# Second rows of the last sums: from VectorE to ScalarE and GpSimd in the closing blocks of an expert layer

## The chip, the cores and the metric

One core of one Trainium2 chip runs the whole program. The metric is the device time of one execution in microseconds; the time before is the median of three runs. A profile is one further execution, recorded by the hardware profiler; its times in this document are microseconds from the start of its span.

## The reference

Four layers follow each other on x of 8 sequences x 512 tokens x 256 features, all in float32:

```python
x = x + attn_a(layernorm(x))      # 16 heads of 64, slopes on the distance, causal
x = x + ffn(layernorm(x))
x = x + attn_b(layernorm(x))      # 8 heads of 128, rotary, causal
x = x + ffn(layernorm(x))

# ffn(x): 8 experts, each token goes to 2 of them
h   = rmsnorm(x) * norm_w
vals, idx = top_k(h @ gate_w.T + gate_b, 2)
wts = softmax(vals)
y_e = mlp2_e(swiglu(mlp1_e(h)))   # for the two experts e of the token
ffn = x + sum(wts[k] * y[idx[k]] for k in (0, 1))
```

The last line of the last layer is what this document is about: to each token's row two expert rows are added, each multiplied by the token's own weight.

## The kernel before, in words

A layer's tokens lie as 8 sequences of 4 tiles, 128 tokens on the partitions and 256 features along them. In an expert layer the 4096 tokens, each with two experts, are sorted by expert into 71 blocks of 128 rows (`TOTAL`). For each block n the loop `Experts.run` issues, in steps:

- `gather` (L939): GpSimd fetches the block's 128 rows from DRAM by an indirect DMA, four blocks ahead (`LEAD`); after step 66 there is none left to fetch;
- `turn_rows` (L953, L961): TensorE transposes, ScalarE copies;
- `first` (L982 to L998), two steps later: TensorE multiplies with the expert's weights, VectorE adds the bias from PSUM (L993), ScalarE takes a sigmoid (L994), and VectorE does three more operations in SBUF (L996, L997, L998);
- `turn_act` (L1007, L1012), then `second` (L1021 to L1033), six steps later (`DEPTH`): TensorE's second product, VectorE's bias from PSUM (L1032, "y"), and GpSimd's indirect DMA that scatters the block's rows to DRAM, to the places of their tokens (L1033, "scatter").

The tokens are sorted in two groups, the first group being sequences 0 to 5. The first 55 blocks (`TOUCHED`) hold all rows of that group, so its results may be read back while the remaining blocks run. The program names blocks by group and number; the second group's numbers 0 to 29 are blocks 41 to 70. This document says y25 or scatter 25 for number 25 of the second group (block 66), and y29 or scatter 29 for the last block.

Reading back goes by halves: two tiles of one sequence, here named by sequence and first tile, 0_0, 0_2, 1_0 and so on to 5_2 for the first group. `collect` (L1078) reads both rows of every token of a half, 256 KB for the first rows and 256 KB for the second. `add` (L1118) makes the sums: for each tile VectorE adds weight times first row to x and then weight times second row to x, two operations of 128x256 that depend on each other. `store` (L1246) sends the half to the output. For half k the three are put at steps n, n + 4 and n + 6 of the loop, with n = 61 + 3k // 2; so the sums of 0_0 and 0_2 stand at 65 and 66, those of 1_0 at 68, and those of 5_2 at 81.

The results of sequences 6 and 7 (second group) can be read only when all scatters are in DRAM. These eight reads, 6_0 to 7_2, are issued last, half on SP's queue (first rows) and half on ScalarE's queue (second rows). In the program text they stand ahead of the sums of 4_0 to 5_2 (steps 77 to 81), and the sums and stores of sequences 6 and 7 close the program.

TensorE's order is written out by hand. On the other engines a scheduler orders the instructions by its own estimates; `keep_in_program_order` holds some of them in the order of the text. Each engine runs its queue in order, and so do SP's queue and ScalarE's queue of DMA issues: whatever waits at the head holds what is behind it. DMAs issued by SP and ScalarE share eight completion semaphores in turn, so that each waits for the one eight places before it. Read buffers are shared: 3_0 takes over the buffer of 1_0, 5_0 that of 3_0, and so on.

Of the kernel before, what the change touches and what calls it, by code (L numbers as in the profile page):

```python
# [41 lines left out]
ALU = mybir.AluOpType  # L42
# [35 lines left out]
TOTAL = (2 * NB * T + SPARE) // P  # L78
# [4 lines left out]
LEAD = 4  # L83
# [10 lines left out]
def layers(  # L94
# [24 lines left out]
    nc = tc.nc  # L119
# [70 lines left out]
    def iota(shape, pattern, name, multiplier=0, base=0, dtype=F32):  # L190
        t = const.tile(shape, dtype, tag=name, name=name)
        nc.gpsimd.iota(
            t,
            pattern=pattern,
            base=base,
            channel_multiplier=multiplier,
            allow_small_or_imprecise_dtypes=True,
        )
        return t
# [6 lines left out]
    tiles = iota([P, 2, NB * NT], [[32, 2], [1, NB * NT]], "tiles", 0, 64)  # L206
# [73 lines left out]
    class Attention:  # L280
# [75 lines left out]
        def scores(self, b, g, n):  # L356
# [4 lines left out]
            if n == 0:  # L361
                rows = []
                for i in range(nh):
                    rows.append(
                        (
                            work.tile([P, PACKED], F32, tag="S", bufs=4, name=f"S_{key}_{i}"),
                            small.tile([P, NT], F32, tag="nm", bufs=4, name=f"nm_{key}_{i}"),
                            small.tile([P, NT], F32, tag="sum", bufs=4, name=f"sum_{key}_{i}"),
                        )
                    )  # L370
                self.S[b, g] = rows
                if kind == "a":
                    add = []
                    for i in range(nh):
                        a = work.tile([P, T], F32, tag="tmp", bufs=3, name=f"ali_{key}_{i}")
                        nc.gpsimd.tensor_scalar(  # L376
                            a, alibi_sb, SLOPES[nh * g + i], 1.0, ALU.mult, ALU.mult
                        )
                        add.append(a)
                    self.add[b, g] = add, -1.0  # L380
                else:
                    self.add[b, g] = [mask_sb], -1.0 / DB
            add, scale = self.add[b, g]
            bank = S_BANKS[n]
            rows = P // nh
# [158 lines left out]
    class Experts:  # L544
# [191 lines left out]
        def blocks_up(self, i, out, counts, add):  # L736

            whole = self.rt(i, [P, NE], "whole", I32)
            nc.vector.tensor_scalar_add(whole, counts, float(add))
            nc.vector.tensor_scalar(  # L740
                whole, whole, 7, 7, ALU.logical_shift_right, ALU.logical_shift_left
            )
            nc.vector.tensor_copy(out, whole)
# [365 lines left out]
                self.read(engines[k], b, got[:, k], k * PLANE + m * P, len(tiles) * P)  # L1109
            self.got[b, tiles[0]] = got  # L1110

        def add(self, b, tiles):
            got = self.got[b, tiles[0]]
            for n, t in enumerate(tiles):
                m = b * NT + t
                xs = X[b][:, t, :]
                for k in range(2):
                    made = nc.vector.scalar_tensor_tensor(  # L1118
                        xs, got[:, k, n, :], self.R["w"][k][:, m : m + 1], xs, ALU.mult, ALU.add
                    )  # L1120
                    tc.keep_in_program_order(made)


# [71 lines left out]
    def flush(left, exp):  # L1195

        turns = (0, 2, 2, 2, 3, 5, 8, 10, 12, 14)
        aside = {}
        for n, piece in zip(turns, left, strict=True):
            aside.setdefault(n, []).append(piece)  # L1200
        for n, piece in zip((16, 18, 20, 22, 25, 28), exp.sorting(1), strict=True):
            aside[n] = [piece]
        return aside
# [7 lines left out]
    att_b, exp_b = Attention("b"), Experts("f2")  # L1211
# [9 lines left out]
    aside = flush(layer(att_a, exp_a, more), exp_a)  # L1221
    aside.setdefault(6, []).append(weights_b)
    aside[done] = [lambda: exp_a.fetch(0)]
    for k, tag in enumerate(("xT", "PT")):
        tt = (2 * k, 2 * k + 1)
# [17 lines left out]
    aside = flush(layer(att_b, exp_b, more), exp_b)  # L1243

    def store(b, tiles, engine):
        engine.dma_start(  # L1246
            out=by_tokens(out[b])[:, tiles[0] : tiles[-1] + 1, :],
            in_=X[b][:, tiles[0] : tiles[-1] + 1, :],
        )
# [7 lines left out]
    for k, (b, tt) in enumerate(halves):  # L1257
        n = done + 3 * k // 2
        tag = ("xT", "PT")[k % 2] if k not in (8, 9) else "qk"
        aside.setdefault(n, []).append(  # L1260
            lambda b=b, tt=tt, tag=tag: exp_b.collect(b, tt, tag, both_queues)
        )
        aside.setdefault(n + 4, []).append(lambda b=b, tt=tt: exp_b.add(b, tt))
        aside.setdefault(n + 6, []).append(lambda b=b, tt=tt: store(b, tt, nc.sync))
    end = TOTAL + DEPTH
    exp_b.run(aside)
# [75 lines left out]
```

## Time and profile before

| | us |
|---|---|
| median of three runs (2226.54 to 2229.31) | 2227.3 |
| the profiled execution, whole | 2239.6 |
| its span, first to last instruction | 2237.8 |
| VectorE's sums in this layer (L1118), 64 operations | 0.480 each (median) |
| the last scatter (L1033), start | 2219.56 |
| the reads of sequences 6 and 7, first issue | 2222.59 |
| the last sum, end | 2234.34 |

How to read the profile: PE is TensorE, PEld its weight loads, DVE VectorE, ACT ScalarE, POOL GpSimd, SP the queue that issues DMAs; ACTq and SPq mark DMA issues on the queue of ScalarE and of SP. A row in order of time has the start, the duration, the engine, the line, the operation and the names of what it writes and reads, the count of merged instructions, and in brackets the idle time of the engine before it and what ended that. Over its span the granted clock of TensorE was 0.993.

### The profile page before, as it was taken

To read this page: it belongs to the slowest core of one execution; us is meant where nothing else is said; L and a number is where in the kernel's file an instruction comes from. 1 tells how busy PE (TensorE), PEld (TensorE's weight loads), DVE (VectorE), ACT (ScalarE), POOL (GpSimd) and SP (SyncE) were. 2 spreads that over 40 slices of the span, in tenths; PEclk is the share of its full clock that TensorE was granted. 3 is DMA by queue.
4 is the path that set the end of the run, shared out by engine and by line. 5 is a ranking of instruction groups with operands and counts; after the bars stand their busy time and mean duration, and the time that the engine had idled before them with its cause. 6 is when DMAs were issued, how large, how long until landed. Compare 5 with 4: busy or idle time off the path is not lost.

```text
span 2237.8 us, 33567 instructions
## 1 busy us (share of the span) xinstructions
PE 2190.3 (98%) x10513; PEld 1429.2 (64%) x10513; DVE 1586.9 (71%) x4817; ACT 961.6 (43%) x2784; POOL 967.1 (43%) x1337
## 2 busy tenths in 40 slices
PE   8999999999999999999999999999999999999995
PEld 5666666666666666656666666666666666665663
DVE  4566666666666687687787676777777678968768
ACT  4555555555555555323324334434444433333331
POOL 5443434243433333266654343333434343356662
PEclk9999999999999999999999999999999999999997
DMA  7100000000000000232220010100101010042237
GB/s 248 39 15 15 6 24 1 30 1 29 1 29 1 29 6 29 99 106 84 90 76 29 10 39 10 39 29 19 48 6 43 6 34 1 19 139 78 85 101 252
DMA packets 78382, 108.80 MB, mean 49 GB/s; under 512 B 9568, under 2 KB 64000, under 8 KB 78208
## 3 DMA queue, kind: packets, MB, share of 16 engines
q1 hardware_dynamic: 62656, 67.58, 9.4%
q0 software_dynamic: 13632, 37.24, 5.4%
q8 instruction: 87, 1.43, 0.3%
q10 hardware_dynamic: 1920, 1.84, 0.3%
q14 instruction: 87, 0.71, 0.1%
HBM read 67.02 MB, written 39.60 MB: 48 GB/s over the span
## 4 chain that ended last, share of the span: by engine, by line
PE 88%; DVE 7%; issue 2%; ACT 1%; POOL 1%; SPq 1%; DMA 1%; DVEq 0%; ACTq 0%; POOLq 0%
PE pp_b L337 10%; PE hp_f L982 9%; PE pp_a L337 9%; PE op_a L476 6%; PE sp_b L395 6%; PE sp_a L395 6%; PE tp_a L449 6%; PE op_b L476 6%; PE yp_a L494 5%; PE yp_b L494 5%; PE vp_a L318 4%; PE y_f L1021 4%; PE vp_b L318 4%; PE tp_b L449 3%; PE gtp_f L953 1%
## 5 line engine op out<-in xcount | busy, mean ns | idle before, releaser
L417 ACT ACTIVATE S_a<-S_a,nm_a 128x512 f32<-128x512 f32 (+3 forms) x512 | 280.1, 548 | 313.7 <-DVE nm_a L407 309.9
L350 POOL TENSOR_TENSOR qk_b<-qk_b,rot_b 128x512 f32<-128x512 f32 x128 | 163.0, 1274 | 453.1 <-DVE qk_b L349 427.7
L376 POOL TENSOR_SCALAR ali_a<-alibi 128x512 f32<-128x512 f32 x128 | 79.3, 620 | 454.9 <-DVE nm_a L407 443.1
L982 PE MATMUL hp_f<-we,hT_f 128*128 x544 | 257.8, 596 | 4.3 <-DVE u_f L993 2.9
L417 ACT ACTIVATE S_b<-S_b,nm_b 128x512 f32<-128x512 f32 (+3 forms) x256 | 142.9, 559 | 241.1 <-DVE nm_b L407 233.4
L407 DVE CUSTOM_DVE_ANT_0 S_a<-sp_a,ali_a 128x512 f32<-128x512 f32 (+3 forms) x512 | 215.9, 487 | 30.7 <-PE sp_a L395 30.7
L434 POOL TENSOR_SCALAR S_a<-S_a,sum_a 128x384 f32<-128x384 f32 x378 | 203.1, 554 | 34.6 <-DVE sum_a L428 25.0
L1033 POOL DMA_INDIRECT y_f<-y_f,row_f x142 | 143.4, 1010 | 114.1 <-DVE y_f L1032 59.2
L407 DVE CUSTOM_DVE_ANT_0 S_b<-sp_b,mask 128x512 f32<-128x512 f32 (+3 forms) x256 | 119.4, 485 | 77.1 <-PE sp_b L395 76.7
L395 PE MATMUL sp_b<-qk_b 128*128 128x512 f32 (+3 forms) x512 | 169.7, 434 | 2.6 <-POOL qk_b L350 2.5
L449 PE MATMUL tp_a<-ident,S_a 128*128 128x128 f32 x1280 | 166.2, 276 | 5.4 <-DVE O_a L484 3.3
L939 POOL DMA_INDIRECT g_f<-h_all_f,token_f x142 | 144.4, 1017 | 59.4 <-issue 39.6
L449 PEld LDWEIGHTS tp_a<-ident,S_a 128*128 128x128 f32 x1280 | 141.3, 142 | 36.8 <-issue 21.3
L994 ACT ACTIVATE u_f<-u_f 128x256 f32<-128x256 f32 x142 | 59.2, 417 | 238.0 <-DVE u_f L993 179.5
L476 PE MATMUL op_a<-PT_a,V_a 128*64 128x384 f32 (+3 forms) x1024 | 156.0, 442 | 3.3 <-ACT S_a L417 2.2
L1021 PEld LDWEIGHTS y_f<-we,aT_f 128*128 128x128 f32 x568 | 108.8, 193 | 77.1 <-issue 59.6
L395 PE MATMUL sp_a<-qk_a 64*128 64x512 f32 (+3 forms) x1024 | 155.5, 443 | 0.9 <-DVE qk_a L354 0.9
L1021 PE MATMUL y_f<-we,aT_f 128*128 x568 | 148.6, 385 | 3.8 <-ACT aT_f L1012 3.7
L459 ACT COPY PT_a<-tp_a 128x512 f32<-128x512 f32 (+1 forms) x320 | 139.1, 496 | 29.4 <-PE tp_a L449 27.6
L476 PE MATMUL op_b<-PT_b,V_b 128*128 128x512 f32 (+3 forms) x512 | 148.7, 433 | 0.0
L993 DVE TENSOR_TENSOR u_f<-hp_f,be 128x512 f32<-128x512 f32 x142 | 98.2, 691 | 59.5 <-PE hp_f L982 20.5
L982 PEld LDWEIGHTS hp_f<-we,hT_f 128*128 128x128 f32 x544 | 92.7, 190 | 73.1 <-issue 66.3
(205 smaller groups left out, 4454.8 us busy)
## 6 DMA issues: line engine op xcount, KB each, us to landing
h_all_f<-hn_f SPq DMA_DIRECT2D x64, 128.0 KB
xm_f<-x_mid_f SPq DMA_DIRECT2D x16, 512.0 KB
yg_f<-y_f SPq DMA_DIRECT2D x32, 256.0 KB
yg_f<-y_f SPq DMA_DIRECT2D x56, 128.0 KB
we<-w_dram SPq DMA_DIRECT2D x8, 512.0 KB
x_mid_f<-x SPq DMA_DIRECT2D x8, 512.0 KB
x_mid_f<-xm_f SPq DMA_DIRECT2D x8, 512.0 KB
x<-x_in_dram SPq DMA_DIRECT2D x7, 512.0 KB
```

The lines of the kernel that those rows point to most:

```text
L318: nc.tensor.matmul(vp[:, k, :], lhsT=self.xT[b][:, c, t * P : (t + 1) * P], rhs=wv[:, c, q * 2 * P : (q + 1) * 2 * P], start=(c == 0), sto ...
L337: nc.tensor.matmul(pp, lhsT=w[:, c, g * P : (g + 1) * P], rhs=self.xT[b][:, c, :], start=(c == 0), stop=(c == NC - 1),)
L350: nc.gpsimd.tensor_tensor(qk[:, j, :], qk[:, j, :], rot, ALU.add)
L395: nc.tensor.matmul(sp[i][:, at[it] : at[it] + w], lhsT=qk[r, 0, it * P : (it + 1) * P], rhs=qk[r, 1, 0:w], start=True, stop=True,)
L407: nc.vector.tensor_tensor_reduce(out=s, in0=sp[i][:, at[it] : at[it] + w], in1=add[i][:, T - w : T], scale=scale, scalar=float(np.finfo(np ...
L417: nc.scalar.activation(s, s, AF.Exp, bias=nm[:, it : it + 1], scale=-1.0, accum_out=sums[:, it : it + 1],)
L434: eng.tensor_scalar(s, s, sums[:, it : it + 1], 1.0, ALU.mult, ALU.mult)
L449: nc.tensor.transpose(tp[:, o : o + P], S[:, S_OFF[it] + jt * P : S_OFF[it] + (jt + 1) * P], ident,)
L476: nc.tensor.matmul(op[i * cols : (i + 1) * cols, jt * P : T], lhsT=v[:, jt, c0 : c0 + cols], rhs=PT[i][:, P_OFF[jt] : P_OFF[jt] + T - jt * P],
L494: nc.tensor.matmul(yp[:, 0:D], lhsT=o[:, c, t * P : (t + 1) * P], rhs=wo[:, half * HALF + c, :], start=(c == 0), stop=(c == HALF - 1),)
L982: nc.tensor.matmul(hp, lhsT=h[:, c * P : (c + 1) * P], rhs=we_sb[:, bass.DynSlice(wat + c * 2 * FI, 2 * FI)], start=(c == 0), stop=(c == N ...
L1021: nc.tensor.matmul(yp, lhsT=aT[:, c * P : (c + 1) * P], rhs=we_sb[:, bass.DynSlice(wat + NC * 2 * FI + c * D, D)], start=(c == 0), stop=(c ...
```

## The change

`add` gets a flag. Where it is set, the second row of each tile is multiplied by its weight in place by ScalarE, and GpSimd adds the product to x. The first row stays with VectorE. The flag is set for halves whose sums stand at step 67 (`TOTAL - LEAD`) or later, from where on no more rows are gathered: 1_0 to 5_2, ten halves of two tiles. The sums of 0_0 and 0_2, those of sequences 6 and 7, and the other expert layer stay as they are.

```diff
-        def add(self, b, tiles):
+        def add(self, b, tiles, shared=False):
             got = self.got[b, tiles[0]]
             for n, t in enumerate(tiles):
                 m = b * NT + t
                 xs = X[b][:, t, :]
                 for k in range(2):
-                    made = nc.vector.scalar_tensor_tensor(
-                        xs, got[:, k, n, :], self.R["w"][k][:, m : m + 1], xs, ALU.mult, ALU.add
-                    )
+                    row, w = got[:, k, n, :], self.R["w"][k][:, m : m + 1]
+                    if k and shared:
+
+                        made = nc.scalar.mul(row, row, w)
+                        tc.keep_in_program_order(made)
+                        nc.gpsimd.tensor_tensor(xs, xs, row, ALU.add)
+                        continue
+                    made = nc.vector.scalar_tensor_tensor(xs, row, w, xs, ALU.mult, ALU.add)
                     tc.keep_in_program_order(made)
...
-        aside.setdefault(n + 4, []).append(lambda b=b, tt=tt: exp_b.add(b, tt))
+        aside.setdefault(n + 4, []).append(
+            lambda b=b, tt=tt, n=n: exp_b.add(b, tt, n + 4 >= TOTAL - LEAD)
+        )
```

## The prediction

> **What bounds the kernel now.** I read the page first, then the busy time by stretches of the end, then the order of time on each engine there. The edit acts only in the second expert layer, from block 67 of 71 on, so the first 2196 us stay as they are. The stretches of the end (PE, PEld, DVE, ACT, POOL busy with counts, then granted clock, DMA share, GB/s):
>
> ```profile
> 2170.00:2190.00 20.00, 20.00 (x82) 12.75 (x82) 15.14 (x37) 6.53 (x20) 12.51 (x13) 1.00 0.67 189
> 2190.00:2210.00 20.00, 18.25 (x71) 11.03 (x69) 18.83 (x47) 5.16 (x16) 5.83 (x6) 1.00 0.77 249
> 2220.00:2238.00 18.00, 0.00 (x0) 0.00 (x0) 13.78 (x32) 0.00 (x0) 0.54 (x1) 0.54 0.78 257
> ```
>
> Until 2190 TensorE is full. After it the sums (L1118) come in and VectorE is full: 18.83 of 20 us, then alone. ScalarE and GpSimd are nearly empty there, but the DMA engines are at 0.78. The order of time shows what ends it (POOL, then DVE, ACT's queue, SP's queue):
>
> ```profile
> 2211.69 1.16 POOL L1033 DMA_INDIRECT y_f<-y_f,row_f  x1 [2.45 <-DVE u_f L996]
> 2215.36 0.97 POOL L1033 DMA_INDIRECT y_f<-y_f,row_f  x1 [0.30 <-issue]
> 2219.56 0.97 POOL L1033 DMA_INDIRECT y_f<-y_f,row_f  x1 [1.74 <-DVE y_f L1032]
> ...
> 2218.87 0.42 DVE L1032 TENSOR_TENSOR y_f<-y_f,be 128x256 f32<-128x256 f32 x1
> 2219.20 15.14 DVE L1118 SCALAR_TENSOR_TENSOR xm_f<-yg_f,wt_f,xm_f 128x256 f32<-128x256 f32 x33
> ...
> 2222.59 2.11 ACTq L1078 DMA_DIRECT2D yg_f<-y_f  x4
> 2230.71 4.05 ACTq L1246 DMA_DIRECT2D out_dram<-xm_f  x2
> ...
> 2222.69 1.92 SPq L1078 DMA_DIRECT2D yg_f<-y_f  x4
> 2227.00 5.91 SPq L1246 DMA_DIRECT2D out_dram<-xm_f  x5
> ```
>
> Two chains meet. One is VectorE's row of sums without a gap. The other is: last y (2218.87), its scatter by GpSimd (2219.56 to 2220.53), landing, and the eight reads of sequences 6 and 7, which wait for every scatter (2222.59, 2.06 us after the scatter's end). Of the 33 sums the last 16 belong to these reads and start at about 2226.9. At 2227.00 SP issues a store that carries a wait for the first of the reads; SP had been free since 2224.61. So the first pair lands about 4.35 us after its issue, just when VectorE comes to it. VectorE and the reads are therefore near a tie: relief for VectorE alone does not move the end unless the last scatter moves as well. From the last sum's end (2234.34) to the end of the span are 3.46 us of store.
>
> **The change part by part.** Twelve halves (two tiles of a sequence) belong to the first stage; halves 1_0 to 5_2, ten of them, change. For each of their 20 tiles one VectorE sum goes, one ScalarE multiplication and one GpSimd addition come.
>
> *VectorE.* The two sums of one tile depend on each other. Start to start they take 0.40 and 0.52 us in turn (33 in 15.14 us is 0.46 on average); first rows alone do not depend on each other, 0.40. So 20 x 0.52 = 10.4 us leave VectorE, 12 of the 20 ahead of the last y, 8 behind it.
>
> *ScalarE.* 20 multiplications of 128x256. Nearest row: the sigmoid of that shape, 0.42 us, so 8.4 us, in two places. Twelve stand between sigmoids and copies, where ScalarE waits 2 to 3 us per block (below): hidden; the copies for the next block come 0.8 us later, and TensorE uses them about 2 us later.
>
> ```profile
> 2200.97 0.42 ACT L994 ACTIVATE u_f<-u_f 128x256 f32<-128x256 f32 x1 [2.79 <-DVE u_f L993]
> ```
>
> The other eight (halves 4_0 to 5_2) stand, in the changed program's order, behind ScalarE's four reads of sequences 6 and 7, and these wait for the last scatter. They cannot start before the reads are out, although their data are there long before. No table load is added.
>
> *GpSimd.* 20 additions. The same form stands in the first layer, undisturbed:
>
> ```profile
> L299 POOL TENSOR_TENSOR x<-x,bout x32: 717/722/732, 13.7 to 795.6; 128x256 f32<-128x256 f32 x32
> ```
>
> They are put between the scatters: after that of y25 come two additions (2_2), scatters 26 and 27, two additions (3_0), scatter 28, two additions (3_2), scatter 29, then eight more. So the last scatter, which gates the reads, now queues behind six additions, each of which waits for ScalarE and VectorE.
>
> *The shared port.* Does a GpSimd addition hold up VectorE? The trace has the case in the attention, a GpSimd operation with a sum beside it:
>
> ```profile
> 1199.53 0.83 POOL L434 TENSOR_SCALAR S_b<-S_b,sum_b 128x384 f32<-128x384 f32 x1
> 1199.83 0.81 DVE L1118 SCALAR_TENSOR_TENSOR xm_f<-yg_f,wt_f,xm_f 128x256 f32<-128x256 f32 x1
> ...
> L1118 DVE SCALAR_TENSOR_TENSOR xm_f<-yg_f,wt_f,xm_f x64: 468/580/809, 1139.8 to 1833.9; 128x256 f32<-128x256 f32 x64
> L1118 DVE SCALAR_TENSOR_TENSOR xm_f<-yg_f,wt_f,xm_f x64: 472/480/486, 2188.0 to 2233.9; 128x256 f32<-128x256 f32 x64
> ```
>
> The sum takes 0.81 instead of 0.48 and ends 0.28 after the GpSimd operation: +0.33 us. At the end of the kernel, with only scatters beside them, no sum is over 0.486. The Trainium skill (SBUF — State Buffer, section "SBUF: two separate sides") states the rule behind it, against this change: a VectorE operation with two SBUF inputs and a GpSimd operation that reads SBUF exclude each other, and the loser "fully blocks". By the rule taken whole, each meeting costs the loser 0.72 us; by the row 0.33, because the start of a sum still overlaps. I take the row and keep 0.72 as the upper end. L997 and L998 also have two SBUF inputs; L993 and L1032 read PSUM and can run beside an addition. The skill's GPSIMD Engine Reference (section "Engine selection") has GpSimd about twice as slow as VectorE with two inputs, that is 0.8 to 1.0 us by this trace's VectorE rows; the row of 0.722 is used.
>
> *Sum.* (a) Up to y25 three changed halves pass (1_0, 1_2, 2_0). A block with four sums takes 3.75 us on VectorE (L993 at 2196.44 to L993 at 2200.19); two second sums less is 1.04, three times 3.1. Two of the six additions meeting a VectorE operation give back 0.6. Scatter 25 starts at 2211.69 - 2.5 = 2209.2. (b) From there to scatter 29 GpSimd has four scatters at 1.27 (0.97 and 0.30 of issue) = 5.1 us and six additions at 0.72 = 4.3, plus 0.2 each for meetings = 1.2: start at 2219.8, against 2219.56. VectorE itself gets to y29 some 5 us earlier than before, for nothing: GpSimd has taken its place. Ends: undisturbed and the full 3.1 earlier, 2218.0; with additions of 1.1 us, 2220.9. Reads then go out at 2222.8, +0.2 us. (c) VectorE is done with the first stage and waits for the pair, 4.35 us, then runs 16 sums, 7.4 us. In this time the last eight additions come: they can start 2.5 us after the reads go out and need at least 5.8 us, so six of them run beside the sums: 6 x 0.33 = +2.0 us (ends: 0, and 6 x 0.72 = 4.3). (d) The stores: that of 6_0 stands on SP's queue ahead of those of 4_0 to 5_2 in the changed order, so eight stores of 256 KB follow the reads where seven did. 0.25 MB at the 257 GB/s above is 1.0 us; I take it as hidden under the longer row of sums, up to 1.0 otherwise.
>
> Sum: +0.2 + 2.0 = +2.2 us. The profiled execution took 2239.6 us (span 2237.8 and 1.8 around it), which becomes 2241.8. The median of the runs shown is 2227.3, 12.3 below the profiled one; the difference is carried over: 2229.5.
>
> **The rivals.** *Faster: VectorE's relief reaches the end.* For it: VectorE is the chain's end for 40 us and loses 10.4. If the additions fit between the scatters, the last scatter follows y29 at about 2214, 5.4 us earlier, and the eight late additions disturb nothing: 2227.3 - 5.4 = 2221.9. Against it: the six additions are ahead of the last scatter in one queue, and (b) leaves at most 1.5 us. It decides if scatter 29 starts before 2216.
>
> *Slower: GpSimd becomes the end.* Each addition waits for two engines and for the port. If one in this stretch takes 1.1 us instead of 0.72, scatter 29 starts at 2220.9 (+1.3); with the late six at the full 0.72 (+4.3) and the eighth store exposed (+1.0) it is +6.6: 2233.9. The point is about 0.9 us per addition together with a whole block per meeting. For it: the queue order and the 0.81 row. Against it: VectorE's PSUM operations leave the port free for 1.1 us of each block.
>
> *The change does not do what it says:* the order on the queues shows twenty multiplications and additions, so no.
>
> **How the numbers follow.** The sum above 0.60, GpSimd and port worse 0.34, relief through 0.06. What a measurement of this kernel can tell from no change is about 0.2%, 4.5 us. Low end: scatter 29 at 2218.0 (-1.5), no meetings, first pair about 1.2 us sooner because fewer stores run beside the reads: -2.7, 2224.5. High end 2234.0, the slower rival whole. Faster 0.06, within 0.60, slower 0.34.
>
> **What would show it.** In the changed profile: 44 sums on VectorE from 2188 on instead of 64; y29 on VectorE before 2215, but scatter 29 at 2219 to 2221 with GpSimd additions right ahead of it; VectorE idle before the 16 last sums, and sums of about 0.8 us among them; the eight late multiplications right behind ScalarE's reads. Wrong if the last scatter starts before 2217 (too pessimistic on GpSimd), if no sum is over 0.5 us (no port), or if the late additions end before the first pair lands.

## The result, and the profile after

The changed kernel took 2233.16 us (median of 13 runs, 2228.49 to 2234.80) beside 2227.3 us for the kernel before in the same session: ratio 1.0019, 95% interval 1.0012 to 1.0026, or +4.2 us (+2.7 to +5.8). The two medians alone lie 5.9 us apart, the means 4.6; the ratio, which is taken over all the runs, is used below. At +4.2 us the loss is just inside the 0.2% that the prediction took as the least that can be told from no change, but the interval shows it to be real; +2.2 us had been forecast.

The profiled execution of the changed kernel ran 10.5 us ahead of that of before when the edit begins, in stages that the edit does not touch. All times below are therefore counted from VectorE's bias addition (L993) of number 25, the last instruction ahead of the first changed half: 2196.44 in the profile before, 2185.93 after. (In the kernel 5_0 takes over the buffer of 2_0, not that of 3_0 as said above, and 5_2 that of 2_2.)

The stretches of the end, in the columns of the same view before (PE, PEld, DVE, ACT, POOL busy and counts, granted clock, DMA share, GB/s):

```profile
2179.50:2199.50 20.00, 19.53 (x78) 12.20 (x76) 19.04 (x42) 7.54 (x22) 9.49 (x11) 1.00 0.78 254
2209.50:2231.70 22.20, 0.00 (x0) 0.00 (x0) 12.51 (x20) 3.30 (x8) 9.57 (x12) 0.50 0.68 224
```

VectorE runs fewer instructions in the first stretch (42, not 47) and is just as full, 19.04 of 20 us: the sums that left came back as longer sums. GpSimd has gone from 5.83 to 9.49 us there and from 0.54 to 9.57 in the last stretch.

The order of time on GpSimd after, from scatter 25 on (start, duration, engine, line, what is written from what, count, idle before it and what ended that):

```profile
2201.16 0.98 POOL L1033 DMA_INDIRECT y_f<-y_f,row_f  x1 [0.76 <-DVE y_f L1032]
2202.16 0.73 POOL L1123 TENSOR_TENSOR xm_f<-xm_f,yg_f 128x256 f32<-128x256 f32 x1
2203.34 0.73 POOL L1123 TENSOR_TENSOR xm_f<-xm_f,yg_f 128x256 f32<-128x256 f32 x1 [0.44 <-DVE xm_f L1125]
2204.22 0.98 POOL L1033 DMA_INDIRECT y_f<-y_f,row_f  x1 [0.15 <-issue]
2205.50 1.22 POOL L1033 DMA_INDIRECT y_f<-y_f,row_f  x1 [0.30 <-DVE xm_f L1125]
2206.75 1.79 POOL L1123 TENSOR_TENSOR xm_f<-xm_f,yg_f 128x256 f32<-128x256 f32 x2
2208.70 0.98 POOL L1033 DMA_INDIRECT y_f<-y_f,row_f  x1 [0.16 <-issue]
2209.71 1.82 POOL L1123 TENSOR_TENSOR xm_f<-xm_f,yg_f 128x256 f32<-128x256 f32 x2
2211.69 0.98 POOL L1033 DMA_INDIRECT y_f<-y_f,row_f  x1 [0.16 <-issue]
2217.13 6.59 POOL L1123 TENSOR_TENSOR xm_f<-xm_f,yg_f 128x256 f32<-128x256 f32 x8 [4.46 <-ACT yg_f L1121]
```

From 2204 on GpSimd never waits for longer than 0.3 us until scatter 29 is out: it is the chain that leads to the last reads. One earlier addition, then the same time on VectorE, ScalarE and SP:

```profile
2198.50 0.73 POOL L1123 TENSOR_TENSOR xm_f<-xm_f,yg_f 128x256 f32<-128x256 f32 x1
...
2198.21 1.32 DVE L1125 SCALAR_TENSOR_TENSOR xm_f<-yg_f,wt_f,xm_f 128x256 f32<-128x256 f32 x1
2205.79 0.41 DVE L1032 TENSOR_TENSOR y_f<-y_f,be 128x256 f32<-128x256 f32 x1
2206.13 6.08 DVE L1125 SCALAR_TENSOR_TENSOR xm_f<-yg_f,wt_f,xm_f 128x256 f32<-128x256 f32 x8
2218.10 10.09 DVE L1125 SCALAR_TENSOR_TENSOR xm_f<-yg_f,wt_f,xm_f 128x256 f32<-128x256 f32 x16 [5.89 <-DMA yg_f<-y_f]
...
2214.46 2.03 ACTq L1078 DMA_DIRECT2D yg_f<-y_f  x4
2216.53 3.30 ACT L1121 ACTIVATE yg_f<-yg_f,wt_f 128x256 f32<-128x256 f32 x8 [12.17 <-issue]
...
2214.49 1.91 SPq L1078 DMA_DIRECT2D yg_f<-y_f  x4
```

The first two lines are the cost in one place. A sum that takes 0.48 us alone takes 1.32 when a GpSimd addition (2198.50 to 2199.23) starts beside it. The next is y29, which starts 5.9 us before its scatter does at 2211.69; before, that gap was 0.7 us. Then come eight sums that take 3.24 us with no addition beside them (seen in the run with memsets below); here, beside four additions, they take 6.08. The last VectorE line is the closing row of 16 sums, 10.09 us instead of 7.4 (2226.93 to 2234.34 before), because seven of the eight late additions lie in it.

| counted from L993 of number 25, us | before | after | difference |
|---|---|---|---|
| scatter 25 starts | 15.25 | 15.23 | 0.0 |
| y29 on VectorE | 22.43 | 19.86 | -2.6 |
| scatter 29 starts | 23.12 | 25.76 | +2.6 |
| last reads, first issue | 26.15 | 28.53 | +2.4 |
| first of the 16 last sums | 30.49 | 32.17 | +1.7 |
| last sum ends | 37.90 | 42.25 | +4.4 |
| span ends | 41.36 | 45.77 | +4.4 |

So the loss has three terms: reads +2.4, the wait from reads to first sum -0.7 (3.64 us instead of 4.34), the last row +2.7.

The block by block gain on VectorE, which the prediction counted on, is read from two L993 in a row. Before, then after:

```profile
2196.44 0.69 DVE L993 TENSOR_TENSOR u_f<-hp_f,be 128x512 f32<-128x512 f32 x1
2200.19 0.69 DVE L993 TENSOR_TENSOR u_f<-hp_f,be 128x512 f32<-128x512 f32 x1
...
2185.93 0.69 DVE L993 TENSOR_TENSOR u_f<-hp_f,be 128x512 f32<-128x512 f32 x1
2189.51 0.68 DVE L993 TENSOR_TENSOR u_f<-hp_f,be 128x512 f32<-128x512 f32 x1
```

The first block with a shared half takes VectorE 3.58 us instead of 3.75.

### The profile page after: what moved, and what is told of

Same layout as the page of the kernel before. It is cut to its first block, busy times and chain, and to the rows that moved or that the text cites. A ratio compares the mean times of both kernels' runs of the same rounds, so it can differ in the third digit from the quotient of the medians.

```text
span 2231.7 us, 33607 instructions
## 1 busy us (share of the span) xinstructions
PE 2184.2 (98%) x10513; PEld 1428.1 (64%) x10513; DVE 1583.6 (71%) x4797; ACT 966.0 (43%) x2804; POOL 979.7 (44%) x1357
## 4 chain that ended last, share of the span: by engine, by line
PE 88%; DVE 6%; ACT 1%; issue 1%; POOL 1%; DMA 1%; SPq 1%; DVEq 0%; ACTq 0%; POOLq 0%
PE hp_f L982 10%; PE pp_b L337 10%; PE pp_a L337 9%; PE op_a L476 6%; PE sp_a L395 6%; PE sp_b L395 6%; PE tp_a L449 6%; PE op_b L476 6%; PE yp_a L494 5%; PE yp_b L494 5%; PE y_f L1021 5%; PE vp_a L318 5%; PE vp_b L318 4%; PE tp_b L449 3%; PE gtp_f L953 1%
## 5 line engine op out<-in xcount | busy, mean ns | idle before, releaser
L993 DVE TENSOR_TENSOR u_f<-hp_f,be 128x512 f32<-128x512 f32 x142 | 98.0, 690 | 73.4 <-PE hp_f L982 67.7
L347 DVE TENSOR_TENSOR rot_b<-pp_b,sin 64x512 f32<-64x512 f32 x128 | 88.7, 693 | 66.6 <-PE pp_b L337 65.3
```

## The experiments

The theory after the result: GpSimd's additions ahead of the last scatter put the reads off, and additions beside VectorE's sums lengthen them through a shared way into SBUF. The rivals: ScalarE's work and its late place; the stores behind the reads; GpSimd's queue alone without any sharing.

The kernel before ran beside each group of these runs, with medians of 2228.6 us (e1 to e4), 2252.0 (e5, e8 to e10) and 2240.4 (e7, e11), so only ratios and times counted from L993 are compared. Microseconds given for a ratio are its excess over 1 times that median. Each run has one trace. How far traces differ by themselves shows in e10, which is the kernel before up to the last 16 sums: its scatter 29 and its reads stand within 0.06 us of those before, its first last sum 0.37 us later. Differences of a few tenths behind the reads therefore prove nothing.

| run | scatter 29 starts | reads | first last sum | row of 16, waits in it included | span ends | ratio to before (95%) |
|---|---|---|---|---|---|---|
| before | 23.12 | 26.15 | 30.49 (no wait) | 7.41 | 41.36 | |
| the change | 25.76 | 28.53 | 32.17 | 10.09 | 45.77 | 1.0019 (1.0012 to 1.0026) |
| e1_late | 22.43 | 27.68 | 31.78 | 9.88 | 45.48 | 1.0011 (1.0003 to 1.0020) |
| e2_early | 25.26 | 28.68 | 32.83 | 7.42 | 43.77 | 1.0012 (1.0006 to 1.0019) |
| e3_mulfirst | 25.98 | 28.74 | 32.73 | 7.42 | 44.14 | 1.0009 (1.0003 to 1.0016) |
| e4_vector_add | 22.92 | 25.89 | 35.29 | 7.42 | 46.14 | 1.0019 (1.0012 to 1.0027) |
| e5_write_only | 22.45 | 25.08 | 29.59 | 7.42 | 40.50 | 0.9999 (0.9990 to 1.0009) |
| e8_left_out | 18.29 | 22.93 | 27.21 | 7.42 | 38.08 | 0.9989 (0.9981 to 0.9997) |
| e9_alternate | 22.77 | 25.84 | 30.23 | 6.81 | 40.72 | 0.9998 (0.9990 to 1.0006) |
| e10_last_alternate | 23.06 | 26.09 | 30.86 | 6.67 | 41.21 | 1.0002 (0.9991 to 1.0014) |
| e7_both | 22.12 | 24.98 | 28.81 | 9.38 | 41.63 | 1.0005 (0.9996 to 1.0013) |
| e11_first_four | 22.20 | 25.82 | 30.23 (no wait) | 7.42 | 41.61 | 1.0003 (0.9995 to 1.0011) |

### Only the late halves shared

```diff
-            lambda b=b, tt=tt, n=n: exp_b.add(b, tt, n + 4 >= TOTAL - LEAD)
+            lambda b=b, tt=tt, n=n: exp_b.add(b, tt, n + 4 >= TOTAL + DEPTH)
```

> Only the halves 4_0 to 5_2 (the eight additions that stand behind scatter 29 in GpSimd's queue) are shared; 1_0 to 3_2 are summed on VectorE as before. Theory (GpSimd's queue before the last scatter, plus slower sums beside late additions): scatter 29 and the last reads at the time of before, counted from the first product of the last but four block; the eight late additions at 0.7 to 0.9 us each meet the 16 last sums, which take about 10 us instead of 7.4; net +1.5 to +2.5 us on before, that is some 2 us less than the full change. Rival 'ScalarE or the stores behind the last reads cause it': all of the +4 us remains, since the eight late multiplications and stores are all still there. Rival 'GpSimd's queue alone': no loss at all, within 0.5 us of before.

The ratio is +2.5 us (+0.7 to +4.5), within what was expected, but not in the way that was expected. The last row took 9.88 us, as forecast. The reads, which were to go out at the time of before, came 1.5 us later, though no addition stood ahead of scatter 29. GpSimd and VectorE in order of time:

```profile
2204.27 1.68 POOL L1033 DMA_INDIRECT y_f<-y_f,row_f  x1 [0.30 <-DVE xm_f L1125]
2206.25 3.59 POOL L1033 DMA_INDIRECT y_f<-y_f,row_f  x1 [0.30 <-DVE xm_f L1125]
...
2205.35 3.64 DVE L1125 SCALAR_TENSOR_TENSOR xm_f<-yg_f,wt_f,xm_f 128x256 f32<-128x256 f32 x9
2215.60 9.88 DVE L1125 SCALAR_TENSOR_TENSOR xm_f<-yg_f,wt_f,xm_f 128x256 f32<-128x256 f32 x16 [6.60 <-DMA yg_f<-y_f]
```

Scatter 29 started 0.7 us earlier than before and took 3.59 us instead of 0.97, to 2209.84. Nine sums stand beside it in one row of 3.64 us, which ends at 2208.99. This was not in the theory; e5, e8 and e9 look at it. The trace ends 4.1 us later than before, which is more than the ratio's 2.5; whether every execution has the long scatter, one trace cannot tell.

### Only the early halves shared

```diff
+            lambda b=b, tt=tt, n=n: exp_b.add(b, tt, TOTAL - LEAD <= n + 4 < TOTAL + DEPTH)
```

> Only the halves 1_0 to 3_2 (the twelve additions ahead of scatter 29 in GpSimd's queue) are shared; 4_0 to 5_2 are summed on VectorE as before. Theory: scatter 29 and the last reads some 2.4 us later than before, the 16 last sums undisturbed at 7.4 us in all, the wait for the first last row 0 to 0.7 us shorter: +1.7 to +2.4 us on before. The two halves of the change together then give about the +4.2 us of the whole. Rival 'the late multiplications, additions and stores cause it all': no loss here.

+2.7 us (+1.3 to +4.2), close to the +1.7 to +2.4 expected, and in the way expected: scatter 29 2.1 us later, reads 2.5 us later, the last row back at its 7.42 us:

```profile
2208.69 0.97 POOL L1033 DMA_INDIRECT y_f<-y_f,row_f  x1 [0.17 <-issue]
...
2216.26 7.42 DVE L1125 SCALAR_TENSOR_TENSOR xm_f<-yg_f,wt_f,xm_f 128x256 f32<-128x256 f32 x16 [2.34 <-DMA yg_f<-y_f]
```

So twelve early additions alone cost the time that the reads lost, with nothing of the change behind the reads.

### The late multiplications ahead of ScalarE's last reads

```diff
+    for m in range(end, n + 7):
+        for piece in aside.get(m, ()):
+            piece()
     for b, tt in last:
         exp_b.collect(b, tt, "S", (nc.sync, nc.scalar))
-    for m in range(end, n + 7):
-        for piece in aside.get(m, ()):
-            piece()
+    for piece in late:          # stores of 4_0 to 5_2
+        piece()
```

> The change as it is, but the eight late multiplications stand ahead of ScalarE's last reads in its order, so that the eight late additions can run while the last reads are on their way; the stores of 4_0 to 5_2 stand behind the reads. Theory: the additions begin right after scatter 29 and are over about when the first last row lands, so most of the 16 last sums run at 0.48 us: the last row of sums takes 7.4 to 8.5 us instead of 10.1, and the time is 1.6 to 2.7 us below the full change, +1.5 to +2.6 on before. If ScalarE's reads come later for it, by more than 0.5 us, that is seen at their issue. Rival 'the late sums are slow for another reason than the additions beside them': still 10 us for the 16, and no gain on the full change.

```profile
2212.13 5.72 POOL L1125 TENSOR_TENSOR xm_f<-xm_f,yg_f 128x256 f32<-128x256 f32 x8
...
2217.89 7.42 DVE L1127 SCALAR_TENSOR_TENSOR xm_f<-yg_f,wt_f,xm_f 128x256 f32<-128x256 f32 x16 [5.38 <-DMA yg_f<-y_f]
```

The eight late additions follow scatter 29 at once, in the time in which VectorE waits for the reads, and end at 2217.85, 0.04 us before the first last sum. The row is 7.42 us. The time is +2.0 us on before (+0.7 to +3.6), where the change had +4.2. In the trace 1.6 us are gained and not the whole 2.7 of the row: the reads go out 0.2 us later than in the change, the first pair follows 0.35 later, and 0.5 us more pass between the last sum and the end, with the stores of 4_0 to 5_2 behind the reads as well. The stretched row is thus the late additions' place beside it, and they had that place because their multiplications stood behind ScalarE's reads.

### VectorE adds the product

```diff
-                        nc.gpsimd.tensor_tensor(xs, xs, row, ALU.add)
+                        made = nc.vector.tensor_tensor(xs, xs, row, ALU.add)
+                        tc.keep_in_program_order(made)
```

> ScalarE multiplies as in the change, VectorE instead of GpSimd adds the product in one two-operand addition. Theory: nothing of the loss comes from ScalarE, so scatter 29 and the reads come as before; the eight late VectorE additions stand ahead of the 16 last sums and wait for ScalarE, whose late multiplications follow its reads (eight at 0.49 us, 3.3 to 4 us after the reads' issue, about when the first last row lands): 0 to +1 us on before. Rival 'ScalarE's multiplications are the cause': +3 to +4 us with no work on GpSimd at all.

A miss: +4.2 us (+2.7 to +6.0). Scatter 29 and the reads stand where they stood before (-0.2 and -0.3 us), with all of ScalarE's early multiplications in: these are not what moves the scatter. The loss is elsewhere:

```profile
2212.67 0.42 DVE L1123 TENSOR_TENSOR xm_f<-xm_f,yg_f 128x256 f32<-128x256 f32 x1 [5.13 <-ACT yg_f L1121]
...
2212.13 3.30 ACT L1121 ACTIVATE yg_f<-yg_f,wt_f 128x256 f32<-128x256 f32 x8 [8.19 <-issue]
```

The first of the late products reaches VectorE 5.13 us after it ran dry, and fifteen operations of the first stage (6.8 us, until 2219.45) stand from there on ahead of the 16 last sums; with products at hand most of them would have been done in the wait. The expectation had overlooked that VectorE holds first-row sums behind an addition that waits. The late place of ScalarE's multiplications is therefore a cost of its own for whoever has to wait for them; in the change itself only GpSimd waits.

### GpSimd writes but reads nothing

```diff
-                        nc.gpsimd.tensor_tensor(xs, xs, row, ALU.add)
+                        for _ in range(2):
+                            nc.gpsimd.memset(row, 0.0)
```

> The change with each GpSimd addition replaced by two memsets of the product's row, which read nothing and touch no sum; the second rows of 1_0 to 5_2 are thereby left out of the sums. ScalarE's multiplications stay as they are. Theory: GpSimd's places ahead of the last scatter remain occupied, by as much as two memsets take (between 0.4 and 1.0 us for the pair by estimate, against 0.72 to 0.95 for an addition), but VectorE's sums no longer slow down where GpSimd works: the 16 last sums take 7.4 us, not 10.1, and no sum takes 0.94. Its first-row sums then follow one another at 0.40 us without a gap. If the reads are put off, it is by GpSimd's queue alone. Rival 'any GpSimd work beside VectorE slows the sums, reading or not': still 0.8 to 0.94 us for the sums beside memsets and about 10 us for the 16. Second question, from the run with late halves alone: whether scatter 29 takes 3 us or more again with eight first-row sums beside it that leave no gap; if that was the sums' doing, it does here too, and the reads come 1.5 us or more later than before.

By source line (count: least/median/most ns), then VectorE and GpSimd in order of time:

```profile
L1126 DVE SCALAR_TENSOR_TENSOR xm_f<-yg_f,wt_f,xm_f x108: 461/484/809, 1145.9 to 2244.0; 128x256 f32<-128x256 f32 x108
L1124 POOL MEMSET yg_f<- x40: 312/325/338, 2210.1 to 2239.3; 128x256 f32 x40
...
2225.11 3.24 DVE L1126 SCALAR_TENSOR_TENSOR xm_f<-yg_f,wt_f,xm_f 128x256 f32<-128x256 f32 x8
2237.09 7.42 DVE L1126 SCALAR_TENSOR_TENSOR xm_f<-yg_f,wt_f,xm_f 128x256 f32<-128x256 f32 x16 [8.74 <-DMA yg_f<-y_f]
...
2227.04 2.17 POOL L1033 DMA_INDIRECT y_f<-y_f,row_f  x1 [0.26 <-DVE xm_f L1126]
2229.95 0.98 POOL L1033 DMA_INDIRECT y_f<-y_f,row_f  x1 [0.17 <-issue]
...
2207.50 0.69 DVE L993 TENSOR_TENSOR u_f<-hp_f,be 128x512 f32<-128x512 f32 x1 [0.26 <-issue]
2210.24 0.68 DVE L993 TENSOR_TENSOR u_f<-hp_f,be 128x512 f32<-128x512 f32 x1
2224.77 0.41 DVE L1032 TENSOR_TENSOR y_f<-y_f,be 128x256 f32<-128x256 f32 x1
```

The 809 ns belongs to the first expert layer, as in the profile before; in the rows of the end the sums follow one another at 0.40 and 0.46 us. ScalarE's late multiplications are in their late place, the stores where they were, and GpSimd has forty memsets in nearly the same order (0.25 us each start to start, so that two take less than one addition). The loss is gone: -0.2 us (-2.3 to +2.0). y29 (2224.77) stands 5.2 us earlier than before, which is the step that the prediction had for the full change (5 us). From L993 of number 25 to that of 26 VectorE takes 2.74 us here, 3.58 in the change and 3.75 before. ScalarE's work and the stores are all there, so they alone do not make the change slower than before; and reading additions, not GpSimd's work as such, slow VectorE. It does not part the queue from the port completely, since the memsets are also shorter and wait for no sum. The 2.17 us is scatter 28, the second long scatter.

The queue still costs here. Scatter 29 starts 5.2 us after y29, and from scatter 26 on GpSimd never waits for longer than 0.30 us: of the 5.2 us by which y29 is earlier than before, 0.7 reach scatter 29. In the next run, with nothing on GpSimd but the scatters, it follows y29 after 2.4 us, and that run is 2.5 us shorter than this one (2249.2 against 2251.7, medians); in the traces its reads go out 2.2 us earlier.

### Second rows left out

```diff
                     if k and shared:
-
-                        made = nc.scalar.mul(row, row, w)
-                        tc.keep_in_program_order(made)
-                        nc.gpsimd.tensor_tensor(xs, xs, row, ALU.add)
                         continue
```

> The second rows of 1_0 to 5_2 are left out of the computation, neither multiplied nor added by any engine: it shows what taking 20 sums off VectorE is worth when nothing is paid for it. 20 sums are 10.4 us of VectorE. By VectorE's relief alone scatter 29 follows y29, some 3.5 us earlier than before, and the time is 3 to 4 us below before. Rival 'sums at 0.40 us without a gap hold off the scatter's issue': scatter 29 starts some 3 us earlier but takes 2 to 4 us instead of 0.97, so that the reads come only 0 to 1.5 us earlier and the gain is under 1.5 us.

-2.5 us (-4.3 to -0.7): between the two expectations. Scatter 29 starts 4.8 us earlier than before, but takes 2.07 us, and the reads follow its end after 2.57 us instead of 2.06, so that they go out 3.2 us earlier:

```profile
2228.11 2.07 POOL L1033 DMA_INDIRECT y_f<-y_f,row_f  x1 [0.30 <-DVE xm_f L1121]
```

This is the ceiling for this order of the work, the longer scatter included: if 10.4 us of VectorE cost nothing at all elsewhere, the kernel would gain about 2.5 us.

### The order of the sums within a half

```diff
-            for n, t in enumerate(tiles):
-                for k in range(2):
+            todo = [(n, k) for n in range(len(tiles)) for k in range(2)]
+            if self.kind == "f2" and b >= 4:
+                todo.sort(key=lambda nk: nk[1])
+            for n, k in todo:
```

> The kernel before, with nothing moved to other engines; only the order of the sums within each half from 4_0 on is changed: first rows of both tiles, then second rows of both, so that no sum follows its own predecessor. Each sum then starts 0.40 us after the last instead of 0.40 and 0.52 in turn: the 16 last sums take 6.5 us instead of 7.4. Theory 'sums without a gap hold off the scatter': scatter 29, which stands beside the 16 sums of 4_0 to 5_2, takes 3 us or more, up to the end of these sums (6 us), and the reads come 2 to 5 us later: +1 to +4 us on before. Rival 'the 3.59 us scatter had another cause' (the depth of its queue, what else was under way): scatter 29 takes 0.97 us as before, and the kernel gains the 0.9 us of the last row.

```profile
2231.59 6.81 DVE L1120 SCALAR_TENSOR_TENSOR xm_f<-yg_f,wt_f,xm_f 128x256 f32<-128x256 f32 x17
2239.41 3.26 DVE L1120 SCALAR_TENSOR_TENSOR xm_f<-yg_f,wt_f,xm_f 128x256 f32<-128x256 f32 x8 [1.01 <-DMA yg_f<-y_f]
2242.97 3.25 DVE L1120 SCALAR_TENSOR_TENSOR xm_f<-yg_f,wt_f,xm_f 128x256 f32<-128x256 f32 x8 [0.30 <-DMA yg_f<-y_f]
...
2231.95 0.97 POOL L1033 DMA_INDIRECT y_f<-y_f,row_f  x1 [1.74 <-DVE y_f L1032]
```

Seventeen sums in a row at 0.40 us each; scatter 29 starts 0.36 us after the first of them, and it takes 0.97 us. A row of sums without a gap is not enough to hold a scatter; that theory falls in this form.

The same order for the last four halves alone (`b >= 6`):

> As the run with the changed order of sums, but only for the last four halves, behind which no scatter stands. Both theories: scatter 29 and reads as before, the 16 last sums in 6.5 us instead of 7.4: 0.9 us below before (about 0.04%, seen in the trace and hardly in the ratio). It also measures what the dependence of a second sum on its first costs by itself. With it the run with both halves' order changed shows what 4_0 to 5_2 do to scatter 29.

Dependence costs 0.12 us per tile, as expected: eight sums take 3.25 us, 16 would take 6.5. But the sums now run ahead of the reads. Between the first eight and the second eight VectorE waits 0.30 us (e9) or 0.16 us (e10) for the next pair, so the row shrinks by 0.6 to 0.7 us instead of 0.9. Neither run can be told from no change: -0.5 us (-2.3 to +1.4) and +0.5 us (-2.0 to +3.2).

### Both orders mended, and four halves only

```diff
+    aside.setdefault(TOTAL - 1 + DEPTH, []).append(additions)   # of 3_0 and 3_2, behind scatter 29
```

with the order of e3 besides: late multiplications ahead of the reads, stores of 3_0 to 5_2 behind them. The last two scatters are held in program order.

> The change with both of its orders mended: the additions of 3_0 and 3_2 stand behind scatter 29 in GpSimd's queue with the other eight, the late multiplications ahead of ScalarE's last reads, the stores of 3_0 to 5_2 behind the reads. Theory (queue ahead of the last scatter, plus additions beside the last sums): scatters 27 to 29 follow one another as before; y29 is done some 2.5 us earlier, but scatter 29 then stands beside ten first-row sums without a gap and may be held to their end, about where it stood before; reads within 1 us of before. Twelve additions at 0.72 us follow it, 8.6 us, of which some 3 us lie beside the last sums: the last row takes 7.4 to 8.5 us. Time 0 to +1.5 us on before, 2.5 to 4 below the change. Rival 'the loss is ScalarE's or the stores': still +3 to +4.

```profile
2220.49 1.20 POOL L1033 DMA_INDIRECT y_f<-y_f,row_f  x1 [0.31 <-DMA yg_f<-y_f]
2221.72 3.56 POOL L1275 TENSOR_TENSOR xm_f<-xm_f,yg_f 128x256 f32<-128x256 f32 x4
2225.24 6.44 POOL L1128 TENSOR_TENSOR xm_f<-xm_f,yg_f 128x256 f32<-128x256 f32 x8
...
2227.18 9.38 DVE L1132 SCALAR_TENSOR_TENSOR xm_f<-yg_f,wt_f,xm_f 128x256 f32<-128x256 f32 x16 [2.47 <-DMA yg_f<-y_f]
```

With the four additions of 3_0 and 3_2 behind it, scatter 29 starts 3.6 us earlier than in the change, 3.9 earlier than in e3, which shares most of the rest of the order, and 1.0 us earlier than before. What those additions cost the queue is thereby shown. The additions then reach 4.5 us into the last row (to 2231.68), and the row is 9.38 us, above the 8.5 that were expected at most. In sum +1.1 us (-0.9 to +2.9), within the range given, about 3 below the change.

```diff
+            lambda b=b, tt=tt, n=n: exp_b.add(b, tt, n + 4 >= TOTAL - LEAD and b < 3)
```

> Only the four halves 1_0 to 2_2 are shared, whose eight additions all stand ahead of scatter 27; 3_0 to 5_2 are summed on VectorE with both rows. Theory: GpSimd has made good its delay by scatter 28, since nothing of the change stands behind scatter 27 in its queue; y29 is done 1 to 2 us earlier and scatter 29 with it; no addition lies beside the last sums: reads 0.5 to 1.5 us earlier, 0.5 to 1.5 us below before. Rival 'any sharing costs, since a sum and an addition that alternate take 0.88 us a pair, no less than two sums on VectorE': y29 no earlier, 0 to +1 us.

+0.7 us (-1.1 to +2.5): no gain, against what was expected. Scatter 29 started 0.9 us earlier, but the reads only 0.3, since they went out 2.65 us after the scatter's end instead of 2.06:

```profile
2223.09 0.97 POOL L1033 DMA_INDIRECT y_f<-y_f,row_f  x1 [0.65 <-issue]
2226.71 2.03 ACTq L1078 DMA_DIRECT2D yg_f<-y_f  x4
...
2222.73 15.81 DVE L1125 SCALAR_TENSOR_TENSOR xm_f<-yg_f,wt_f,xm_f 128x256 f32<-128x256 f32 x35
```

VectorE ran without a gap from y29 to the last sum. With 35 sums behind y29 instead of 33, that sum ended only 0.25 us earlier than before, and the span ended 0.25 us later. Of the versions that keep the work whole, none measurably beats the kernel before.

What is left of the theories: the stores and ScalarE's early work do not cause the loss (e4, e5). ScalarE's late place is a condition of the longer last row (e3), not a cost by itself in the change. That the queue ahead of the last scatter puts the reads off is shown by e2 and e7, and by what is left in e5; that additions beside sums lengthen them, by e3 and e5. The queue alone does not do: it does not say why the last row takes 10.09 us with additions beside it and 7.42 without (e3), nor why a sum takes 1.32 us beside an addition and 0.48 beside memsets (e5). How much of the +2.4 us at the reads is the queue and how much the longer sums, no run parts exactly.

## Why the prediction was right or wrong

The call, a kernel slower by less than the 0.2% that can be told from no change, was right, and so was the mechanism: scatter 29 behind GpSimd's additions, late additions beside the last row. The size was half of what was measured, +2.2 against +4.2 us. Of the signs that it named, the 44 sums, the sums of 0.83 to 0.94 us in the last row, VectorE's wait ahead of it and the late multiplications right behind the reads came as said. Two came late: moved to the times of the profile before, y29 stands at 2216.3 and scatter 29 at 2222.2, where the prediction had y29 before 2215 and the scatter at 2219 to 2221.

(a) is the step that failed. It had scatter 25 come 2.5 us earlier; scatter 25 came at the same time as before (15.23 against 15.25). A block with a shared half took VectorE 3.58 us against 3.75, a gain of 0.17 where 1.04 had been counted; over the three halves 0.4 us were gained, and they were lost again because y25 now stood behind L996 and no longer ahead of it. The mis-sized term is the price of a meeting: 0.33 us was taken from the one row with a partial overlap (0.81), but a sum that starts while an addition is at work or about to start took 1.32, which is +0.84, and every shared half of the early blocks had one (1.04 less 0.84 is 0.20, near the 0.17). GpSimd's second addition then waited 0.44 us for that very sum. With memsets in the additions' place the block took 2.74 us, 1.0 less than before, as (a) had it without meetings. That operations on PSUM run beside an addition held: L993 took 0.68 us with an addition beside it (2199.45, against 2199.67 to 2200.39), 0.69 before.

The rule that the prediction weighed and took only as its upper end was nearer here. The Trainium skill (SBUF — State Buffer, "SBUF: two separate sides") gives the shared ports to the instruction that starts first, for the whole of it, and lets the other block. The early meetings cost the sum 0.84 us, more than the 0.72 of an addition, though the sum is recorded as starting first (2198.21, the addition at 2198.50) and would by the rule have had the ports. In the long rows the cost is less than the rule gives: where sums and additions alternate, sums take 0.83 to 0.94 us and additions about 0.90, one pair every 0.87 us. If they excluded each other whole, a pair would take about 1.1 us, 0.40 and 0.68, the steps at which sums and additions (e3) each follow their own kind. The two sums of a tile on VectorE alone take 0.92. So beside additions a shared tile is worth next to nothing to VectorE's time, and the addition is paid besides.

(b) held. From scatter 25 to scatter 29 the prediction had 10.6 us; it was 10.53 (2201.16 to 2211.69), as four scatters, six additions and some waits. Because (a) gave no lead, scatter 29 came 2.6 us late instead of 0.2. VectorE's y29, forecast 5 us earlier, was 2.6 earlier, and as forecast for nothing.

(c) was short in one term and long in another, and the two cancelled by chance. The wait from reads to first sum was 3.64 us instead of 4.35; the prediction had a shorter wait in its low end only. The 16 sums took +2.7 instead of +2.0: seven of them met additions, not six, at some 0.38 each. ScalarE's multiplications took 0.49 us, not 0.42.

(d) held: from the last sum to the end of the span about 3.5 us in both profiles, with eight stores behind the reads.

Sum of what was missed: +2.4 (a), -0.3 because the reads followed the last scatter's end after 1.79 us instead of 2.06, -0.7 and +0.7 (c), so +2.2 becomes +4.3; the trace has +4.4. Of the rivals, "GpSimd becomes the end" is close to what happened in the queue, though not by its price: it had additions of 1.1 us, and they took 0.73 to 0.95; what was longer were the sums. "Relief reaches the end" would have been worth 5.4 us by the prediction; even with nothing paid elsewhere it is about 2.5 (e8), since the last scatter and the reads took back 1.6 us of the scatter's lead.

## What to carry to other kernels

Before work is moved from VectorE to GpSimd, price one meeting of the two from the fastest alternation that the moved work itself will make, not from a chance overlap elsewhere: here a sum and an addition that both read SBUF took nearly as long as two sums (0.87 us against 0.92). Look next at what is queued behind the moved work on its new engines, here the scatter that gates the last reads and ScalarE's reads ahead of the multiplications. And ask first what the relief is worth with its cost left out: one run of that kind gave the ceiling, 2.5 us or a quarter of the VectorE time removed.

## What the runs showed of the hardware

*A write-only GpSimd operation does not disturb VectorE's sums.* Sums beside memsets (0.325 us each) took 0.48; beside additions of the same shape, 0.83 to 1.32. The Trainium skill (SBUF — State Buffer, "Who interferes with whom") names reading by GpSimd as the condition for a VectorE operation with two SBUF inputs, and this trace agrees.

*A scatter seems to be held by VectorE's sums.* Three scatters of some 2 to 4 us were seen where every other one of this kernel takes 0.96 to 1.7. All three end 0.84 to 0.86 us after the end of the row of sums beside them: 2209.84 against 2208.99 (e1, 3.59 us), 2229.21 against 2228.35 (e5, 2.17 us), 2230.18 against 2229.34 (e8, 2.07 us). An undisturbed scatter takes 0.97, so all but its first 0.12 us seems to wait for the row. The same distance stands behind shorter delays, of one sum each: scatters of 1.15 and 1.22 us in e8 (2225.14, 2226.59) and of 1.22 us in the change (scatter 27, 2205.50) end 0.85 us after the end of the one sum that was running when they started. In e9 and before, scatter 29 starts 0.36 us into a sum that has 0.11 to 0.12 us left, and 0.97 us is just what a wait for that sum alone gives; so e9 does not speak against a hold by the running sum. Why three scatters waited out the whole row and others one sum stays open: all of them followed on other work of GpSimd after 0.26 to 0.30 us of idle time, and the 2.17 us of e5 began 0.35 us into a sum, as the scatter of e9 did. No run tested it.

*The reads follow the last scatter's end after 1.65 to 2.65 us*, and where VectorE waits for their first pair, it waits until 3.6 to 4.8 us after issue. Neither was explained by the runs; each moves the end by up to a microsecond, as much as some of the differences sought here.
